# Two graph layers on one core: where the weights of later stages are loaded and prepared

## The chip, the cores and the metric

The kernel runs on 1 core of one Trainium2 chip. The metric is device time in microseconds, lower is better. The core has a matrix engine (TensorE, PE in the profile), a vector engine (VectorE, DVE), an engine for activation functions (ScalarE, ACT), GpSimd (POOL) and SyncE (SP), which here only issues DMA transfers. ScalarE and GpSimd issue transfers too; an engine's issues stand in the profile under its queue (SPq, ACTq, POOLq).

## The reference

Two graph layers run one after the other on 16 graphs of 1024 nodes with 256 features, all in float32, each followed by a residual sum and a layer norm over the features:

```
layer 0:  h = x W                        4 heads of 64
          e[i,j] = sum over t of (adj==t+1) * (a_src[t].h[i] + a_dst[t].h[j]),  leaky_relu, masked where adj == 0
          out = relu(softmax(e) h + bias) + h;  norm over each head's 64;  x = norm(x + out)
layer 1:  n = norm(x) * gamma1 + beta1;  scores = n n^T / sqrt(32), 8 heads of 32, masked where adj <= 0
          x2 = x + softmax(scores) n
          y  = norm(x2) * gamma2 + beta2;  out = x2 + gelu(y W1 + b1) W2 + b2;  x = norm(x + out)
```

W is 256 x 256 in all, W1 256 x 1024, W2 1024 x 256. adj holds 0 and 1 here, so of the five types t only the first counts; the kernel's fast path uses that (index 0 of the last axis of a_src and a_dst) and keeps a verdict whether its assumptions held.

## The kernel before, in words

Layer 0 of batch b has two stages. `prepare` (L286) takes the 1024 nodes in four pairs of blocks of 128: x is transposed on TensorE (`transpose_rows`, L222), the adjacency is transposed and turned into a mask (`turn_mask`, L290), and each block is multiplied by `w0e` (L322). `w0e` holds W and, beside it, 8 columns W a_src and W a_dst, so that one product gives h and both attention terms. ScalarE takes the product out of PSUM (L323 to L327), and VectorE adds the bias (`take_h`, L347). `attention0` (L350) then runs 16 steps: each has VectorE compute four weight tiles p (L374) and TensorE 32 products with them (L389; a float32 product gives two records). The tiles p lie in 4 buffers, two of them used by one step, and step i+1's p are computed beside step i's products. Every second head, `spread_factor` (L357; products L363, ScalarE L365) makes the factors cb for the next heads. After each head, `after0` (L432) divides and, after the last head of a half of 512 rows, runs the norms as a chain of short pieces. Layer 1 is `attention1` (L502), `finish1` and `mlp` (L629), which uses `w1_sb`, `w2_sb` and `b1_sb`.

The order on TensorE, ScalarE, VectorE and GpSimd is written out by hand for the main part (`manual_schedule`, L760): two generators, `layer0()` and `layer1()`, are advanced in turn. Each `yield` states a cost, which moves a clock; chains (`begin(chain, wait)`) are resumed when the clock reaches their time, and `complete(chain)` runs one to its end. The clock only fixes the order of instructions; the hardware then runs each engine's list in that order, with waits on semaphores. A batch of layer 1 begins when layer 0 of that batch is handed over. SyncE isn't among the engines ordered by hand: the framework orders its issues by itself, and it did so in the head of the program (before L760) for all engines.

The head, L111 to L193: constants; `w0e` is loaded by ScalarE's queue in 8 pieces (L141); then for a_src and for a_dst, one after the other, the vector is loaded into a buffer that both share (L148; 640 KB, as every partition gets a copy), multiplied by W on VectorE (L154) and summed over each head (L155) into w0e. After these, ScalarE's queue loads columns (L165), rows spread over all partitions (L159: biases, norm weights, b2), and w1, w2 and b1 (L178, L180, L182; w1 and w2 1 MB each). Then the weights are prepared: b2 - beta1 (L176), w1 times beta2 on TensorE (L188, 16 products with one column each), added to b1 (L191), and w1 scaled by gamma2 (L193, twice 128x1024). Pools named one, two, three, four and six have that many buffers for each name; `ps_o` is a pool of two PSUM banks that attention 1 and the MLP also use.

Of the kernel before, what the change touches and what calls it, by code (L numbers as in the profile page):

```python
# [31 lines left out]
F32 = mybir.dt.float32  # L32
# [4 lines left out]
OP = mybir.AluOpType  # L37
# [13 lines left out]
def fast_path(  # L51
# [56 lines left out]
    ps_o = ctx.enter_context(tc.tile_pool(name="ps_o", bufs=2, space=PSUM))  # L108


    ident = const.tile([P, P], F32, name="ident")  # L111
    make_identity(nc, ident)
    identb = const.tile([P, P], BF16, name="identb")
# [29 lines left out]
    apart = [const.tile([P, H0, Q], F32, name=f"apart{g}") for g in range(GB)]  # L143
    for t in apart:
        nc.vector.memset(t, 0.0)
    for src, dst in ((a_src, w0e[:, :, D + H0 : D + 2 * H0]), (a_dst, w0e[:, :, D : D + H0])):
        a = one.tile([P, H0, HO, T], F32, name="v0")
        nc.scalar.dma_start(  # L148
            a.rearrange("p h e t -> p (h e t)"),
            bass.AP(tensor=src.tensor, offset=src.offset, ap=[[0, P], [1, H0 * HO * T]]),  # L150
        )
        for c in range(DC):
            t = two.tile([P, H0, HO], F32, name="z")
            nc.vector.tensor_mul(t, w0e[:, c, 0:D].rearrange("p (h e) -> p h e", e=HO), a[:, :, :, 0])  # L154
            nc.vector.tensor_reduce(dst[:, c, :], t, axis=mybir.AxisListType.X, op=OP.add)  # L155

    def rows(src, name):
        t = const.tile([P, D], F32, name=name)
        nc.scalar.dma_start(t, bass.AP(tensor=src.tensor, offset=src.offset, ap=[[0, P], [1, D]]))  # L159
        return t  # L160

    columns = []
    for name, src in (("g1_c", gamma1), ("be1_c", beta1), ("g2_c", gamma2), ("be2_c", beta2)):
        t = const.tile([P, DC], F32, name=name)
        nc.scalar.dma_start(t, src.rearrange("(c p) -> p c", p=P))  # L165
        columns.append(t)
    bias0_r = rows(bias0, "bias0_r")
    nbias0_r = rows(bias0, "nbias0_r")
    nc.vector.tensor_scalar(nbias0_r, nbias0_r, -1.0, None, op0=OP.mult)
    lng0_r = rows(lng0, "lng0_r")  # L170
    lnb0_r = rows(lnb0, "lnb0_r")
    g1_r = rows(gamma1, "g1_r")
    be1_r = rows(beta1, "be1_r")

    b2_r = rows(b2, "b2_r")
    nc.vector.tensor_sub(b2_r, b2_r, be1_r)  # L176
    w1_sb = const.tile([P, DC, DFF], F32, name="w1_sb")
    nc.scalar.dma_start(w1_sb, w1.rearrange("(c p) f -> p c f", p=P))  # L178
    w2_sb = const.tile([P, FC, D], F32, name="w2_sb")
    nc.scalar.dma_start(w2_sb, w2.rearrange("(c p) d -> p c d", p=P))  # L180
    b1_sb = const.tile([P, FC], F32, name="b1_sb")
    nc.scalar.dma_start(b1_sb, b1.rearrange("c p -> p c"))  # L182

    g1_c, be1_c, g2_c, be2_c = columns
    pb = ps_o.tile([P, FC], F32, name="po")
    for f in range(FC):
        for c in range(DC):
            nc.tensor.matmul(  # L188
                pb[:, f : f + 1], w1_sb[:, c, f * P : (f + 1) * P], be2_c[:, c : c + 1], start=c == 0, stop=c == DC - 1
            )  # L190
    nc.vector.tensor_add(b1_sb, b1_sb, pb)  # L191
    for c in range(DC):
        nc.vector.tensor_scalar(w1_sb[:, c, :], w1_sb[:, c, :], g2_c[:, c : c + 1], None, op0=OP.mult)  # L193


    def power(src, n, name):
# [57 lines left out]
    def advance(cost):  # L254
        clock[0] += cost
        for item in list(chains):
            if item[0] <= clock[0]:
                run(item)
# [370 lines left out]
    def mlp(b, halves):  # L629


        chunks = [(n, q) for n in range(NH) for q in range(0, BPH, GB)]

        def first(yT, q, f, hid):
            ph = ps_s.tile([P, GB * P], F32, name="ps")
            for c in range(DC):
                nc.tensor.matmul(  # L637
                    ph,
                    w1_sb[:, c, f * P : (f + 1) * P],
                    yT[:, c, q * P : (q + GB) * P],  # L640
                    start=c == 0,
                    stop=c == DC - 1,
                )
            nc.scalar.activation(hid[f // 4][:, f % 4, :], ph, AF.Gelu, bias=b1_sb[:, f : f + 1], scale=1.0)  # L644

        def second(n, q, g, hid, x1):
            k = n * BPH + q + g
            po = ps_o.tile([P, D], F32, name="po")
            for f in range(FC):
                nc.tensor.matmul(  # L650
                    po,
                    hid[f // 4][:, f % 4, g * P : (g + 1) * P],
                    w2_sb[:, f, :],
                    start=f == 0,
                    stop=f == FC - 1,
                )
            begin(last_norm(b, k, po, x1[:, q + g, :]), 1.5)

        before = []
        for n, q in chunks:  # L660
            complete(halves[n][2])
            x1, yT, _ = halves[n]
            hid = []
            for f in range(FC):
                if f % 4 == 0:
                    hid.append(three.tile([P, 4, GB * P], F32, name="hid"))
                first(yT, q, f, hid)
                if f % 2 == 1:
                    yield 1.75
                    if f < 2 * GB and before:  # L670
                        second(*before.pop(0))
                        yield 3.5
            before = [(n, q, g, hid, x1) for g in range(GB)]
        for part in before:
            second(*part)
            yield 3.5
# [42 lines left out]
    def layer1():  # L719
        for b in range(B):  # L720
            place[1][:] = b, 0.0
            seen, rinv1, mask = handed.pop(b)

            def half(n):
                finish_norms(b, n)
                return handed[b, n]

            yT = [two.tile([P, DC, HALF], F32, name="yT") for _ in range(NH)]
            halves = {}

            def done(n, o, heads):
                x1 = handed[b, n][0]
                chain = finish1(o, x1, yT[n], heads)
                halves[n] = x1, yT[n], chain
                begin(chain, 6.0)

            yield from attention1(half, mask, rinv1, done)
            yield from mlp(b, halves)
            in_range(seen)

# [15 lines left out]
    for i in range(3):  # L756
        load_adj(i)
    load_blocks(0)
    E = mybir.EngineType
    with tc.manual_schedule(engines={E.PE, E.Activation, E.DVE, E.Pool}):  # L760
        streams = [layer0(), layer1()]
        while any(streams):
            lead = streams[0] and (place[0][0] + place[0][1] / WORK0 < wanted() or not streams[1])
            which = 0 if lead else 1
            cost = next(streams[which], None)
            if cost is None:
                streams[which] = None
            else:
                place[which][1] += cost
                advance(cost)  # L770
        while chains:
            run(chains[0])
    right = const.tile([P, B * NB], F32, name="right")
    nc.vector.tensor_scalar(right, types, N / 2 + 2.0, None, op0=OP.is_lt)
    nc.vector.tensor_reduce(ok, right, axis=mybir.AxisListType.X, op=OP.min)
# [442 lines left out]
```

## Time and profile before

| | before |
|---|---|
| time, median of 3 runs | 3663.64 us (3661.22 to 3666.74) |
| span of the profiled run | 3660.5 us, mean granted TensorE clock 0.985 |
| busy PE, DVE, ACT, POOL | 94%, 82%, 59%, 11% |
| first product at L322 | starts at 36.26 us |
| first weight tile of attention 0 (L374) | starts at 63.77 us |
| first product of attention 1 (L517) | starts at 134.03 us |
| landing of w1 and w2, from their issue | 9.2 and 11.2 us |

How to read the profile: "busy" is time with at least one instruction of that engine at work. A timeline line gives start, length, engine, line, operation, what it writes and reads, shapes, a count of merged instructions, and in brackets the idle time before it and what ended that. The chain of waits goes back from the last instruction, at each step to what released it. A wait for several things is put down to the one that came last. The granted clock of TensorE is a share of full speed.

### The profile page before, as it was taken

What the parts mean: (1) busy time and instruction counts of PE and PEld (TensorE: products, weight loads), DVE (VectorE), ACT (ScalarE), POOL (GpSimd) and SP (SyncE); (2) the same over time, 40 slices, a digit from 0 to 9 for tenths busy, and PEclk for the clock granted to TensorE, in tenths of its full rate; (3) what the DMA queues carried; (4) which work ended last, traced back from release to release, by engine and by line L of the source; (5) the groups of instructions that cost most, each with busy time, mean ns of one, the idle gap of its engine ahead of it and who ended that gap; (6) DMA issues with size and microseconds to landing.
All of it is one profiled execution on the core that took longest, in us unless ns stands there. A gap on an engine that the chain in (4) does not pass through costs nothing.

```text
span 3660.5 us, 142025 instructions
## 1 busy us (share of the span) xinstructions
PE 3452.5 (94%) x64417; PEld 2304.6 (63%) x64417; DVE 2986.7 (82%) x5328; ACT 2156.0 (59%) x4732; POOL 384.5 (11%) x360
## 2 busy tenths in 40 slices
PE   5699999999999999999999999999999999999998
PEld 4458476575766757566585765757667575665846
DVE  4888788887878888788887988888788887888884
ACT  2474846647466574755747566474665747557464
POOL 0101101010110101101011010101101011010110
PEclk9799999999999999999999999999999999999999
DMA  4110201102010110201102011020101102010000
GB/s 106 28 23 16 46 6 42 18 26 36 13 41 12 33 29 14 45 7 38 23 16 46 6 40 20 26 36 13 41 12 32 31 14 45 7 38 9 16 6 14
DMA packets 77669, 97.67 MB, mean 27 GB/s; under 512 B 9088, under 2 KB 60160, under 8 KB 77056
## 3 DMA queue, kind: packets, MB, share of 16 engines
q0 software_dynamic: 18432, 33.56, 6.4%
q1 hardware_dynamic: 52736, 50.35, 4.4%
q8 instruction: 506, 8.29, 0.9%
q10 hardware_dynamic: 5888, 4.60, 0.4%
q14 instruction: 107, 0.88, 0.1%
HBM read 105.26 MB, written 16.78 MB: 33 GB/s over the span
## 4 chain that ended last, share of the span: by engine, by line
PE 63%; DVE 26%; issue 4%; ACT 3%; POOL 3%; DMA 1%; ACTq 0%; SPq 0%; DVEq 0%; POOLq 0%
PE ps L517 13%; PE po L535 10%; PE ps L637 9%; PE acc L389 9%; DVE p L528 7%; PE po L650 7%; PE po L542 6%; DVE p L374 6%; PE acc L322 3%; POOL r L198 3%; DVE st L203 2%; PE acc L295 1%; PE acc L227 1%; PE ps L363 1%; DVE mv L204 1%
## 5 line engine op out<-in xcount | busy, mean ns | idle before, releaser
L528 DVE TENSOR_TENSOR p<-p,mask 128x1024 f32<-128x1024 f32 x1024 | 1199.1, 1218 | 160.7 <-ACT p L522 156.9
L522 ACT ACTIVATE p<-ps 128x512 f32<-128x512 f32 x2048 | 1059.6, 614 | 329.6 <-PE ps L517 327.8
L517 PE MATMUL ps<-nT 32*128 32x512 f32 x4096 | 769.1, 654 | 12.6 <-ACT cb L365 10.0
L374 DVE SCALAR_TENSOR_TENSOR p<-cb,dinv,mask 128x512 f32<-128x512 f32 x1024 | 698.4, 744 | 0.5 <-ACT cb L365 0.5
L542 PEld LDWEIGHTS po<-v,p 128*32 128x32 f32 x32768 | 390.0, 110 | 334.2 <-issue 239.5
L389 PE MATMUL acc<-v,p 128*64 128x65 f32 x16384 | 556.4, 225 | 43.8 <-DVE p L374 42.7
L389 PEld LDWEIGHTS acc<-v,p 128*64 128x64 f32 x16384 | 511.5, 139 | 118.0 <-DVE p L374 65.2
L644 ACT ACTIVATE hid<-ps,b_sb 128x256 f32<-128x256 f32 x512 | 235.5, 471 | 555.4 <-PE ps L637 555.1
L535 PE MATMUL po<-p,v 128*32 128x512 f32 x2048 | 550.2, 612 | 10.4 <-DVE p L528 8.9
L535 PE MATMUL po<-p,unit 128*32 128x512 f32 x2048 | 549.5, 612 | 0.0
L637 PE MATMUL ps<-yT,w_sb 128*128 128x256 f32 x2048 | 491.6, 387 | 0.7 <-issue 0.7
L650 PE MATMUL po<-w_sb,hid 128*128 128x256 f32 x2048 | 465.0, 381 | 0.0
L650 PEld LDWEIGHTS po<-w_sb,hid 128*128 128x128 f32 x2048 | 385.4, 190 | 64.0 <-issue 11.4
L637 PEld LDWEIGHTS ps<-yT,w_sb 128*128 128x128 f32 x2048 | 376.2, 191 | 64.3 <-issue 12.2
L542 PE MATMUL po<-v,p 128*32 128x33 f32 x32768 | 387.6, 198 | 7.5 <-DVE o L584 3.1
L517 PEld LDWEIGHTS ps<-nT 32*128 32x128 f32 x4096 | 268.0, 186 | 170.8 <-issue 56.8
L535 PEld LDWEIGHTS po<-p,v 128*32 128x32 f32 x2048 | 78.7, 109 | 387.5 <-DVE p L528 204.5
L198 POOL TENSOR_TENSOR r<-v,mhalf 128x1 f32<-128x1 f32 (+1 forms) x160 | 158.1, 988 | 1009.2 <-DVE v L684 721.7
L296 ACT ACTIVATE mask<-acc,shift_c 128x1024 uint8<-128x1024 bf16 x128 | 144.3, 1127 | 44.3 <-PE acc L295 43.8
L322 PE MATMUL acc<-w0e,xT 128*128 128x264 f32 x512 | 146.2, 409 | 20.9 <-DVE hb L347 20.8
L278 POOL DMA_DIRECT2D ak<-in_adj_dram x128 | 69.7, 545 | 878.1 <-PE acc L295 864.7
L198 POOL TENSOR_TENSOR r<-v1s,mhalf 128x4 f32<-128x4 f32 x32 | 34.9, 1092 | 1132.2 <-DVE ranges L418 891.0
(116 smaller groups left out, 2929.2 us busy)
## 6 DMA issues: line engine op xcount, KB each, us to landing
ak<-in_adj_dram POOLq DMA_DIRECT2D x128, 256.0 KB, 3.9
xk<-in_x_dram SPq DMA_DIRECT2D x64, 256.0 KB, 2.8
xl<-in_x_dram SPq DMA_DIRECT2D x32, 512.0 KB, 4.0
out_dram<-z SPq DMA_DIRECT2D x128, 128.0 KB, 1.7
w_sb<-in_L_gnn_W_dram ACTq DMA_DIRECT2D x2, 1024.0 KB, 10.2
v<-in_L_gnn_a_src_dram ACTq DMA_DIRECT2D x1, 640.0 KB, 7.8
v<-in_L_gnn_a_dst_dram ACTq DMA_DIRECT2D x1, 640.0 KB, 3.8
w0e<-in_L_gnn_W_dram ACTq DMA_DIRECT2D x8, 32.0 KB, 7.3
```

Of the source, the lines that this page charges most:

```text
L198: nc.gpsimd.tensor_tensor(r, src, mhalf[:, :n], op=OP.pow)
L322: nc.tensor.matmul(ph, xT[:, c, g * P : (g + 1) * P], w0e[:, c, :], start=c == 0, stop=c == DC - 1)
L374: nc.vector.scalar_tensor_tensor(p[:, i, :], cb[:, hd % PAIR, :], dinv[:, j2 + i, hd : hd + 1], mask[n][:, j2 + i, :], op0=OP.max, op1=OP. ...
L389: nc.tensor.matmul(av[at : at + TILE, q, :], ps[i // 2][:, i % 2, q * P + at : q * P + at + TILE], v0[:, j4 + i, hd, :], start=j4 + i == 0 ...
L517: nc.tensor.matmul(tiles[e], of_keys[q, quad, keys], of_queries[q, quad, :], start=True, stop=True)
L522: nc.scalar.activation(p[:, i, :], tiles[e + i], AF.Exp, scale=SCALE1)
L528: nc.vector.tensor_mul(p, p, mask[n][:, jb, None, :].to_broadcast([P, PAIR, HALF]))
L535: nc.tensor.matmul(moved[at * Q : (at + 1) * Q, :], v, ps[0][:, e, :], start=jb == 0, stop=jb == NB - 1)
L542: nc.tensor.matmul(held[at : at + Q, q, e, :], ps[1][:, e, q * P + at : q * P + at + Q], values[:, hd, :], start=jb == 0 and e == 0 and q ...
L637: nc.tensor.matmul(ph, w1_sb[:, c, f * P : (f + 1) * P], yT[:, c, q * P : (q + GB) * P], start=c == 0, stop=c == DC - 1,)
L644: nc.scalar.activation(hid[f // 4][:, f % 4, :], ph, AF.Gelu, bias=b1_sb[:, f : f + 1], scale=1.0)
L650: nc.tensor.matmul(po, hid[f // 4][:, f % 4, g * P : (g + 1) * P], w2_sb[:, f, :], start=f == 0, stop=f == FC - 1,)
```

## The change

The weights that only layer 1 and the end of layer 0 need are no longer loaded by ScalarE's queue in the head, but by SyncE, and what is computed from them becomes a chain, `later_weights`, that is begun with the first batch and runs in pieces beside it; `complete(weights_of_later)` stands ahead of the MLP as a safeguard. The order by hand now starts at the beginning of the program, so the head too is in program order on the four engines. The attention vectors no longer share one buffer one after the other: their four halves (two heads each) lie in the buffers of `v0` and `xl`, which nothing else needs yet; a_src is loaded by SyncE and a_dst by ScalarE. The multiplication by W is done for two heads at a time. The bias row is loaded once, and its negative computed from it. What it is for: the first batch should not wait for weights of later stages, nor a_dst for a_src.

```diff
--- before.py
+++ after.py
@@ -108,6 +108,10 @@
     ps_o = ctx.enter_context(tc.tile_pool(name="ps_o", bufs=2, space=PSUM))
 
 
+    E = mybir.EngineType
+    ctx.enter_context(tc.manual_schedule(engines={E.PE, E.Activation, E.DVE, E.Pool}))
+
+
     ident = const.tile([P, P], F32, name="ident")
     make_identity(nc, ident)
     identb = const.tile([P, P], BF16, name="identb")
@@ -143,54 +147,76 @@
     apart = [const.tile([P, H0, Q], F32, name=f"apart{g}") for g in range(GB)]
     for t in apart:
         nc.vector.memset(t, 0.0)
-    for src, dst in ((a_src, w0e[:, :, D + H0 : D + 2 * H0]), (a_dst, w0e[:, :, D : D + H0])):
-        a = one.tile([P, H0, HO, T], F32, name="v0")
-        nc.scalar.dma_start(
-            a.rearrange("p h e t -> p (h e t)"),
-            bass.AP(tensor=src.tensor, offset=src.offset, ap=[[0, P], [1, H0 * HO * T]]),
-        )
+    terms = ((a_src, nc.sync, w0e[:, :, D + H0 : D + 2 * H0]), (a_dst, nc.scalar, w0e[:, :, D : D + H0]))
+
+    at = one.tile([P, 3, PAIR, HO, T], F32, name="v0")
+    vectors = [at[:, i, :, :, :] for i in range(3)] + [one.tile([P, PAIR, HO, T], F32, name="xl")]
+    for i, (src, queue, _) in enumerate(terms):
+        for pair in range(H0 // PAIR):
+            queue.dma_start(
+                vectors[i * PAIR + pair].rearrange("p h e t -> p (h e t)"),
+                bass.AP(
+                    tensor=src.tensor,
+                    offset=src.offset + pair * PAIR * HO * T,
+                    ap=[[0, P], [1, PAIR * HO * T]],
+                ),
+            )
+
+    def rows(queue, src, name):
+        t = const.tile([P, D], F32, name=name)
+        queue.dma_start(t, bass.AP(tensor=src.tensor, offset=src.offset, ap=[[0, P], [1, D]]))
+        return t
+
+    bias0_r = rows(nc.scalar, bias0, "bias0_r")
+    for i, (_, _, dst) in enumerate(terms):
         for c in range(DC):
             t = two.tile([P, H0, HO], F32, name="z")
-            nc.vector.tensor_mul(t, w0e[:, c, 0:D].rearrange("p (h e) -> p h e", e=HO), a[:, :, :, 0])
+            for pair in range(H0 // PAIR):
+                heads = slice(pair * PAIR, (pair + 1) * PAIR)
+                nc.vector.tensor_mul(
+                    t[:, heads, :],
+                    w0e[:, c, pair * P : (pair + 1) * P].rearrange("p (h e) -> p h e", e=HO),
+                    vectors[i * PAIR + pair][:, :, :, 0],
+                )
             nc.vector.tensor_reduce(dst[:, c, :], t, axis=mybir.AxisListType.X, op=OP.add)
-
-    def rows(src, name):
-        t = const.tile([P, D], F32, name=name)
-        nc.scalar.dma_start(t, bass.AP(tensor=src.tensor, offset=src.offset, ap=[[0, P], [1, D]]))
-        return t
-
-    columns = []
-    for name, src in (("g1_c", gamma1), ("be1_c", beta1), ("g2_c", gamma2), ("be2_c", beta2)):
-        t = const.tile([P, DC], F32, name=name)
-        nc.scalar.dma_start(t, src.rearrange("(c p) -> p c", p=P))
-        columns.append(t)
-    bias0_r = rows(bias0, "bias0_r")
-    nbias0_r = rows(bias0, "nbias0_r")
-    nc.vector.tensor_scalar(nbias0_r, nbias0_r, -1.0, None, op0=OP.mult)
-    lng0_r = rows(lng0, "lng0_r")
-    lnb0_r = rows(lnb0, "lnb0_r")
-    g1_r = rows(gamma1, "g1_r")
-    be1_r = rows(beta1, "be1_r")
-
-    b2_r = rows(b2, "b2_r")
-    nc.vector.tensor_sub(b2_r, b2_r, be1_r)
+    nbias0_r = const.tile([P, D], F32, name="nbias0_r")
+    nc.vector.tensor_scalar(nbias0_r, bias0_r, -1.0, None, op0=OP.mult)
+
+    lng0_r, lnb0_r, g1_r, be1_r, b2_r = [
+        const.tile([P, D], F32, name=name) for name in ("lng0_r", "lnb0_r", "g1_r", "be1_r", "b2_r")
+    ]
+    g1_c, be1_c, g2_c, be2_c = [const.tile([P, DC], F32, name=name) for name in ("g1_c", "be1_c", "g2_c", "be2_c")]
     w1_sb = const.tile([P, DC, DFF], F32, name="w1_sb")
-    nc.scalar.dma_start(w1_sb, w1.rearrange("(c p) f -> p c f", p=P))
     w2_sb = const.tile([P, FC, D], F32, name="w2_sb")
-    nc.scalar.dma_start(w2_sb, w2.rearrange("(c p) d -> p c d", p=P))
     b1_sb = const.tile([P, FC], F32, name="b1_sb")
-    nc.scalar.dma_start(b1_sb, b1.rearrange("c p -> p c"))
-
-    g1_c, be1_c, g2_c, be2_c = columns
-    pb = ps_o.tile([P, FC], F32, name="po")
-    for f in range(FC):
+
+    def later_weights():
+        for t, src in ((lng0_r, lng0), (lnb0_r, lnb0), (g1_r, gamma1), (be1_r, beta1), (b2_r, b2)):
+            nc.sync.dma_start(t, bass.AP(tensor=src.tensor, offset=src.offset, ap=[[0, P], [1, D]]))
+        for t, src in ((g1_c, gamma1), (be1_c, beta1), (g2_c, gamma2), (be2_c, beta2)):
+            nc.sync.dma_start(t, src.rearrange("(c p) -> p c", p=P))
+        nc.sync.dma_start(b1_sb, b1.rearrange("c p -> p c"))
+        yield 6.0
+        nc.sync.dma_start(w1_sb, w1.rearrange("(c p) f -> p c f", p=P))
+        nc.sync.dma_start(w2_sb, w2.rearrange("(c p) d -> p c d", p=P))
+        yield 24.0
+
+        nc.vector.tensor_sub(b2_r, b2_r, be1_r)
+
+        pb = ps_o.tile([P, FC], F32, name="po")
+        for f in range(FC):
+            for c in range(DC):
+                nc.tensor.matmul(
+                    pb[:, f : f + 1],
+                    w1_sb[:, c, f * P : (f + 1) * P],
+                    be2_c[:, c : c + 1],
+                    start=c == 0,
+                    stop=c == DC - 1,
+                )
+        yield 3.5
+        nc.vector.tensor_add(b1_sb, b1_sb, pb)
         for c in range(DC):
-            nc.tensor.matmul(
-                pb[:, f : f + 1], w1_sb[:, c, f * P : (f + 1) * P], be2_c[:, c : c + 1], start=c == 0, stop=c == DC - 1
-            )
-    nc.vector.tensor_add(b1_sb, b1_sb, pb)
-    for c in range(DC):
-        nc.vector.tensor_scalar(w1_sb[:, c, :], w1_sb[:, c, :], g2_c[:, c : c + 1], None, op0=OP.mult)
+            nc.vector.tensor_scalar(w1_sb[:, c, :], w1_sb[:, c, :], g2_c[:, c : c + 1], None, op0=OP.mult)
 
 
     def power(src, n, name):
@@ -735,6 +761,7 @@
                 begin(chain, 6.0)
 
             yield from attention1(half, mask, rinv1, done)
+            complete(weights_of_later)
             yield from mlp(b, halves)
             in_range(seen)
 
@@ -756,20 +783,20 @@
     for i in range(3):
         load_adj(i)
     load_blocks(0)
-    E = mybir.EngineType
-    with tc.manual_schedule(engines={E.PE, E.Activation, E.DVE, E.Pool}):
-        streams = [layer0(), layer1()]
-        while any(streams):
-            lead = streams[0] and (place[0][0] + place[0][1] / WORK0 < wanted() or not streams[1])
-            which = 0 if lead else 1
-            cost = next(streams[which], None)
-            if cost is None:
-                streams[which] = None
-            else:
-                place[which][1] += cost
-                advance(cost)
-        while chains:
-            run(chains[0])
+    weights_of_later = later_weights()
+    begin(weights_of_later, 3.0)
+    streams = [layer0(), layer1()]
+    while any(streams):
+        lead = streams[0] and (place[0][0] + place[0][1] / WORK0 < wanted() or not streams[1])
+        which = 0 if lead else 1
+        cost = next(streams[which], None)
+        if cost is None:
+            streams[which] = None
+        else:
+            place[which][1] += cost
+            advance(cost)
+    while chains:
+        run(chains[0])
     right = const.tile([P, B * NB], F32, name="right")
     nc.vector.tensor_scalar(right, types, N / 2 + 2.0, None, op0=OP.is_lt)
     nc.vector.tensor_reduce(ok, right, axis=mybir.AxisListType.X, op=OP.min)
```

## The prediction

> **What bounds the kernel now.** I read the page first, then the chain that ended last in order of time for the first 140 us, then the timeline of the same stretch, and last the sums by stage and the waits. The page says which engine carries the whole run:
>
> ```profile
> span 3660.5 us, 142025 instructions
> ...
> PE 3452.5 (94%) x64417; PEld 2304.6 (63%) x64417; DVE 2986.7 (82%) x5328; ACT 2156.0 (59%) x4732; POOL 384.5 (11%) x360
> ...
> PE 63%; DVE 26%; issue 4%; ACT 3%; POOL 3%; DMA 1%; ACTq 0%; SPq 0%; DVEq 0%; POOLq 0%
> ```
>
> TensorE bounds the body, and the change shortens nothing there. It touches the head, where little else can run: layer 1 needs layer 0 of batch 0, which needs the product at L322. So a microsecond off the start of the first L322 moves all later work by as much, unless it is given back. The chain of the first stretch (start, length, what):
>
> ```profile
> 1.78 10.14 DMA xl<-in_x_dram
> ...
> 18.05 2.03 ACTq L159
> 20.12 9.24 DMA w_sb<-in_L_gnn_W_dram
> 29.41 6.99 PE po L188 x32
> 36.40 1.98 PE acc L322 x4
> ```
>
> The last wait before the first L322 is the load of w1 (9.24 us), then the 16 products at L188 (32 matmul records, 6.99 us). L322 uses neither; they are merely ahead of it on TensorE. The timeline of the same stretch shows when its own inputs were there:
>
> ```profile
> 1.78 0.46 SPq L269 DMA_DIRECT2D xl<-in_x_dram  x1
> ...
> 6.11 0.69 ACTq L148 DMA_DIRECT2D v<-in_L_gnn_a_src_dram  x1
> ...
> 15.25 0.35 ACTq L148 DMA_DIRECT2D v<-in_L_gnn_a_dst_dram  x1
> ...
> 19.11 1.14 DVE L154 TENSOR_TENSOR z<-w0e,v 128x256 f32<-128x256 f32 x2 [3.11 <-DMA v<-in_L_gnn_a_dst_dram]
> ...
> 24.14 1.28 ACT L230 ACT_TABLE_LOAD   x1 [24.14 <-DMA lnb_r<-in_L_gnn_ln_beta_dram]
> ...
> 36.26 2.11 PE L322 MATMUL acc<-w0e,xT 128*128 128x264 f32 x4
> ```
>
> w0e was complete at 20.9 us (L154 from 19.11, L155 to 20.91), ScalarE computed nothing before 24.14 because it was still issuing loads, and L322 started at 36.26. Sums of two stretches (us, PE, PEld, DVE, ACT, POOL, clock, DMA share, GB/s):
>
> ```profile
> 5.00:10.00 5.00, 0.00 (x0) 0.10 (x1) 0.00 (x0) 0.00 (x0) 0.00 (x0) 1.00 1.00 213
> 64.00:112.00 48.00, 39.16 (x908) 31.05 (x908) 47.58 (x91) 4.42 (x8) 0.00 (x0) 1.00 0.01 3
> ```
>
> Before 14 us the DMA engines are the limit. From 64 to 112 us, attention of layer 0 for batch 0, VectorE is (47.58 of 48 us) and TensorE has 9 us free: that is where the moved work lands.
>
> **What the Trainium skill says.** "DMA: Bandwidth & Descriptors", section "Issuing engines are not separate DMA queues": loads from any engine share the same 16 DMA engines and interleave. The trace agrees: share 1.00 from 5 to 10 us with three issuers. So moving loads to SyncE frees ScalarE's time, but the bytes ahead of L322 decide. "TensorE: Matmul & The Clock Gate", Part 1: the array runs at half clock until it has been busy for a window of about 3.4 us, and falls back after an idle one. Here the same two L322 products took 2.11 us at 36.26 and 1.16 us from 40.12 on, so the head runs cold; the records also show clock 0.59 from 120 to 140 us, after TensorE pauses.
>
> **The change, part by part.**
> *w1, w2, rows, columns and b1 leave ScalarE's queue; L188, L191, L193 and L176 leave the head.* Removed from the path: all between w0e being ready and L322. What remains:
> 1. Bytes. Up to the landing of a_src at 13.9 us (6.11 + 7.8 to landing), w0e 0.26 MB, xk 2 x 0.26, xl 0.52, ak 3 x 0.26 and a_src 0.66 had been asked for: 2.75 MB. The rates of the windows (162, 213, then 232 GB/s) give 2.78 MB by then, so this is bandwidth. After the change both vectors must be there (2 x 0.66), and xl can't be fetched early, since its buffer holds half of a_dst: 2.89 MB, landing at 13.9 + 0.14/0.232 = 14.5 us. Loads behind them on SyncE mix in. SyncE isn't in the hand-written order (the xl load of a much later step went out at 1.78), so rows and w1, w2 will go out early too, whatever the place of their chain. None of it mixed in: 14.5. The five rows wholly ahead (0.66 MB): 17.3. w1 and w2 too (2.1 MB at 252 GB/s): 25.6. I take 15, since a_dst sits in ScalarE's queue near its front and w1, w2 are SyncE's last.
> 2. VectorE after that landing: for a_dst two chunks of two half multiplies and a reduce. A half is not in the trace; the whole L154 is 609 ns and a 128x64 operation (L421) 276, so 276 to 609; I take 350. 2 x (2 x 350 + 409) = 2.2 us.
> 3. ScalarE issues 8 + 2 + 1 loads; with waits for earlier landings until 11 to 12 us, then 1.3 for the table and 1.7 for xT and the first mask: ready at 15, hidden behind 17.
>
> So L322 starts at 15 + 2.2 = 17.2 instead of 36.26: 19.1 us less (bounds 14.5 + 1.7 and 25.6 + 2.9: from 20.1 to 7.8 less).
> *The second bias load* (0.13 MB) goes; the negation (282 ns) waits for the one left, hidden behind ScalarE's L323 to L327, for which VectorE waits anyway (up to 3.4 us at L347).
> *The prepared weights come back inside attention 0.* By the yields (13 for prepare, 1 + 1, then 2 a step) the chain, due 24 after 9.75, runs at clock 35, after step 9; its last part at 39. VectorE gets L176 424 + L191 155 + 2 x 751 = 2.1 us, all on the path, as VectorE has no gap there. TensorE gets L188: 6.99 us cold, and 3.5 if the warm clock halves it. Behind it on TensorE stand these (products, spread factors), and VectorE waits for the buffers that they free:
>
> ```profile
> 96.87 2.67 PE L389 MATMUL acc<-v,p 128*64 128x65 f32 x64 [1.42 <-DVE p L374]
> ...
> 99.47 1.13 PE L363 MATMUL ps<-esr,spread 32*128 32x512 f32 x4
> ```
>
> Step 9 ends at 95.44. With L188, then two steps of 2.0 us and 1.13 for L363, TensorE is through step 11 at 104.1 to 107.6, and VectorE, which has the 2.4 us of L445 and L446 to do here, needs those buffers at about 108.5; the factor (cb) for step 12 is wanted at 105.6 and comes at 103.2 to 106.7. So 0 to 1.1 us; I take 0.3.
> *w1 and w2 beside prepare* (2.1 MB, 8 us of DMA in some 26) slow the loads of adj and x; prepare runs at a DMA share of 0.65 and ScalarE is its bound (16.36 of 20 us), with adj three blocks ahead. 0 to 3 us; I take 0.2.
> Sum: -19.1 + 2.1 + 0.3 + 0.2 = -16.5 us; 3663.6 - 16.5 = 3647.
>
> **Rivals.**
> *A, the loads collide.* w1 and w2 get ahead of a_dst, and L322 starts near 26 (-10.3), with 2.1 + 1 given back: about -7, 3657. For it: SyncE fetches greedily, and loads wait for landings of unrelated ones:
>
> ```profile
> SPq L269 <- DMA w0e<-in_L_gnn_W_dram: 10.4, 1, 10.4
> ```
>
> A load of x there waited for w0e, because (so the records) eight completion semaphores go round among all loads of SyncE and ScalarE. Against it: that same rule holds w1 back until the ninth load before it or so has landed.
> *B, the hand-over warms up.* From 129.9 to 166 us some 16 us of TensorE work on the chain ran at half clock. If the shifted pauses let it run warm, up to 8 us more: 3639. Against it: the pauses come from VectorE's chain and shift with it.
> *C, slower.* L322 near 28 (-8), prepare cold throughout for want of L188's burst (12.73 us of TensorE in 20 would become 25, so 26 us become 33: +7), x blocks stuck behind w1 and w2 in SyncE's queue (+5), 2.1 + 1 given back: +7, 3671. Against it: a TensorE that is full when cold warms itself, and L188 for 7 us didn't warm it either (L322 after it was cold).
>
> **How the numbers follow.** Main case 0.68, A 0.12, B 0.14, C 0.06. The time is that of the main case, 3647. Its own bounds (L322 from 16.2 to 20.2, prices) give 3645 to 3651, a few us more for clock windows and for the spread of the runs before (3661 to 3667). With part of A and B the range is 3638 to 3656. 0.2% is 7.3 us, so faster means below 3656.3: main and B nearly whole, a third of A: 0.86; same 0.08; slower 0.06.
>
> **What would show it.** First L322 at 16 to 20 us, with VectorE's multiply of a_dst as its releaser. ScalarE's table load near 12. L188 near 76 us, between two L389 groups, taking 3.5 to 7 us with no gap on VectorE behind it; VectorE's work of attention 0 longer by 2.1. The first L517 at about 117.5 instead of 134.03, and the rest of the timeline the same distance ahead. It is wrong if L322 waits for a_dst beyond 22, if prepare takes over 28 us, or if the gap at the first L517 differs from that at the end.

## The result, and the profile after

| | before | after |
|---|---|---|
| time, median of 4 runs | 3663.93 us (3661.22 to 3666.74) | 3648.76 us (3646.30 to 3652.41) |
| ratio to before, 95% interval | | 0.9959 (0.9942 to 0.9977) |
| span of the profiled run | 3660.5 us | 3649.4 us |
| first product of W and x done (ScalarE's first copy out of it) | 38.40 | 21.48 |
| first weight tile of attention 0 | 63.77 | 46.87 |
| first product of attention 1 | 134.03 | 119.36 |

The kernel is 15.2 us faster; 3647 us had been forecast. Lines have moved: L322 is now L348, L188 L209, L374 L400, L389 L415, L517 L543, L154 L176. The page of the profile after, its totals and shares of the chain:

```profile
span 3649.4 us, 142033 instructions
...
PE 3449.4 (95%) x64417; PEld 2302.3 (63%) x64417; DVE 2988.7 (82%) x5332; ACT 2155.9 (59%) x4732; POOL 384.4 (11%) x360
...
PE 64%; DVE 25%; issue 4%; ACT 3%; POOL 3%; DMA 1%; SPq 0%; ACTq 0%; POOLq 0%; DVEq 0%
```

Busy times are those of before to some 3 us: nothing was saved in work, only in waiting. The chain of waits in order of time (start, length, what) for the head and the place where the prepared weights come back:

```profile
0.76 4.32 DMA w0e<-in_L_gnn_W_dram
5.10 7.79 DMA w0e<-in_L_gnn_W_dram
12.90 5.33 DMA xl<-in_L_gnn_a_dst_dram
...
73.22 5.32 PE acc L415 x128
78.55 4.77 PE po L209 x32
83.32 3.66 PE acc L415 x64
86.98 1.48 PE ps L389 x4
88.49 0.61 ACT cb L391
```

w1 (9.24 us) and L188 (6.99 us) are gone from the head. In their place stands a_dst, and ahead of it W. The timeline of the same stretch:

```profile
9.56 0.33 ACTq L156 DMA_DIRECT2D v<-in_L_gnn_a_dst_dram  x1
...
12.90 0.33 ACTq L156 DMA_DIRECT2D xl<-in_L_gnn_a_dst_dram  x1
...
14.06 1.28 ACT L256 ACT_TABLE_LOAD   x1 [14.06 <-DMA v<-in_L_gnn_a_dst_dram]
...
18.25 0.39 DVE L176 TENSOR_TENSOR z<-w0e,xl 128x128 f32<-128x128 f32 x1 [3.33 <-DMA xl<-in_L_gnn_a_dst_dram]
...
18.72 0.51 SPq L295 DMA_DIRECT2D xk<-in_x_dram  x1
...
19.20 2.25 PE L348 MATMUL acc<-w0e,xT 128*128 128x264 f32 x4 [8.52 <-issue]
19.28 0.47 SPq L200 DMA_DIRECT2D w_sb<-in_L_gnn_W_dram  x1
```

The second half of a_dst was issued only at 12.90, when the sixth piece of W had landed, and was there at 18.24. L348 began at 19.20 with the part of w0e that was ready and waited inside for the last reduce. SyncE sent the third x load just ahead of w1 here. And the place of the prepared weights, with VectorE's only wait of that stretch:

```profile
78.48 4.84 PE L209 MATMUL po<-be_c,w_sb 128*128 128x1 f32 x32
...
83.25 3.73 PE L415 MATMUL acc<-v,p 128*64 128x65 f32 x64
...
89.12 2.74 DVE L400 SCALAR_TENSOR_TENSOR p<-cb,dinv,mask 128x512 f32<-128x512 f32 x4 [0.40 <-ACT cb L391]
```

### The profile page after: what moved, and what is told of

The parts are those of the page before. It is cut to its first block, busy times and chain, and to the rows that moved or that the text cites. A ratio compares the mean times of both kernels' runs of the same rounds, so it can differ in the third digit from the quotient of the medians.

```text
span 3649.4 us, 142033 instructions
## 1 busy us (share of the span) xinstructions
PE 3449.4 (95%) x64417; PEld 2302.3 (63%) x64417; DVE 2988.7 (82%) x5332; ACT 2155.9 (59%) x4732; POOL 384.4 (11%) x360
## 3 DMA queue, kind: packets, MB, share of 16 engines
q10 hardware_dynamic: 1584, 1.05, 0.1%
## 4 chain that ended last, share of the span: by engine, by line
PE 64%; DVE 25%; issue 4%; ACT 3%; POOL 3%; DMA 1%; SPq 0%; ACTq 0%; POOLq 0%; DVEq 0%
PE ps L543 13%; PE po L561 10%; PE ps L663 9%; PE acc L415 9%; DVE p L554 7%; PE po L676 7%; PE po L568 6%; DVE p L400 6%; PE acc L348 3%; POOL r L224 3%; DVE st L229 2%; PE acc L321 1%; PE acc L253 1%; PE ps L389 1%; DVE mv L230 1%
## 5 line engine op out<-in xcount | busy, mean ns | idle before, releaser
L543 PE MATMUL ps<-nT 32*128 32x512 f32 x4096 | 770.1, 655 | 12.6 <-ACT cb L391 10.0
L400 DVE SCALAR_TENSOR_TENSOR p<-cb,dinv,mask 128x512 f32<-128x512 f32 x1024 | 698.5, 744 | 0.9 <-ACT cb L391 0.9
L415 PE MATMUL acc<-v,p 128*64 128x65 f32 x16384 | 556.1, 226 | 42.1 <-DVE p L400 40.1
L415 PEld LDWEIGHTS acc<-v,p 128*64 128x64 f32 x16384 | 512.0, 139 | 114.3 <-DVE p L400 61.6
L561 PE MATMUL po<-p,v 128*32 128x512 f32 x2048 | 548.3, 610 | 10.5 <-DVE p L554 8.8
L543 PEld LDWEIGHTS ps<-nT 32*128 32x128 f32 x4096 | 268.2, 186 | 171.1 <-issue 56.9
L348 PE MATMUL acc<-w0e,xT 128*128 128x264 f32 x512 | 146.4, 409 | 29.5 <-DVE hb L373 20.9
L322 ACT ACTIVATE mask<-acc,shift_c 128x1024 uint8<-128x1024 bf16 x128 | 144.3, 1127 | 43.6 <-PE acc L321 42.8
```

Source lines behind the costliest of these rows:

```text
L348: nc.tensor.matmul(ph, xT[:, c, g * P : (g + 1) * P], w0e[:, c, :], start=c == 0, stop=c == DC - 1)
L400: nc.vector.scalar_tensor_tensor(p[:, i, :], cb[:, hd % PAIR, :], dinv[:, j2 + i, hd : hd + 1], mask[n][:, j2 + i, :], op0=OP.max, op1=OP. ...
L415: nc.tensor.matmul(av[at : at + TILE, q, :], ps[i // 2][:, i % 2, q * P + at : q * P + at + TILE], v0[:, j4 + i, hd, :], start=j4 + i == 0 ...
L543: nc.tensor.matmul(tiles[e], of_keys[q, quad, keys], of_queries[q, quad, :], start=True, stop=True)
L561: nc.tensor.matmul(moved[at * Q : (at + 1) * Q, :], v, ps[0][:, e, :], start=jb == 0, stop=jb == NB - 1)
```

## Experiments

All stages below are read in one profile per run: "product" is ScalarE's first copy out of the first product of W and x, "tile" VectorE's first weight tile, "attention 1" TensorE's first product of it. The time from product to tile is prepare, from tile to attention 1 attention 0; the body is from there to TensorE's last product.

| run | median us | ratio to before (95%) | product | tile | attention 1 | prepare | attention 0 | body |
|---|---|---|---|---|---|---|---|---|
| before | | | 38.40 | 63.77 | 134.03 | 25.4 | 70.3 | 3518 |
| the change | 3648.76 | 0.9959 (0.9942-0.9977) | 21.48 | 46.87 | 119.36 | 25.4 | 72.5 | 3522 |
| the change, again | 3650.54 | 0.9963 (0.9951-0.9975) | 24.67 | 52.40 | 124.38 | 27.7 | 72.0 | 3515 |
| the change, third | 3652.39 | 0.9962 (0.9948-0.9976) | 23.69 | 51.41 | 123.89 | 27.7 | 72.5 | 3522 |
| weights only | 3659.51 | 0.9988 (0.9981-0.9994) | 31.84 | 57.26 | 129.73 | 25.4 | 72.5 | 3518 |
| buffers only | 3664.52 | 1.0001 (0.9993-1.0010) | 39.12 | 64.49 | 134.75 | 25.4 | 70.3 | 3515 |
| no products | 3662.20 | 0.9992 (0.9984-1.0001) | 22.91 | 50.63 | 122.55 | 27.7 | 71.9 | 3531 |
| other products | 3652.57 | 0.9956 (0.9941-0.9971) | 23.68 | 49.08 | 121.51 | 25.4 | 72.4 | 3522 |
| products at start | 3652.86 | 0.9957 (0.9942-0.9973) | 24.02 | 50.38 | 122.32 | 26.4 | 71.9 | 3521 |
| type 0 alone | 3654.68 | 0.9967 (0.9955-0.9979) | 22.63 | 48.02 | 120.49 | 25.4 | 72.5 | 3521 |
| W in two loads | 3646.17 (one run) | | 16.88 | 46.43 | 118.43 | 29.6 | 72.0 | 3518 |
| all of it | 3650.48 | 0.9954 (0.9940-0.9967) | 14.83 | 44.40 | 115.59 | 29.6 | 71.2 | 3520 |
| late loads | 3650.56 | 0.9956 (0.9942-0.9969) | 18.02 | 46.70 | 118.70 | 28.7 | 72.0 | 3520 |
| all, late | 3646.69 | 0.9942 (0.9928-0.9956) | 15.09 | 42.80 | 113.12 | 27.7 | 70.3 | 3523 |

Beside the first pair, the runs come from two chips. The medians of before on them were 3664.38 (again, weights only, buffers only, no products) and 3667.16 to 3667.97 (the rest), so times are compared by their ratios. Runs of one kernel spread over 5 to 7 us; differences of a few microseconds are read in the stages, not in the totals.

### The two halves of the change apart

Weights only: the vectors share one buffer again, each in one load on ScalarE's queue. The order by hand from the start of the program and the single load of the bias row stay as in the change; what these two do was not tried apart.

```diff
-    at = one.tile([P, 3, PAIR, HO, T], F32, name="v0")
-    vectors = [...]
...
+    for src, _, dst in terms:
+        a = one.tile([P, H0, HO, T], F32, name="v0")
+        nc.scalar.dma_start(a.rearrange("p h e t -> p (h e t)"), ...)
```

> The later weights moved as in the change, but a_src and a_dst still share one buffer, one load each on ScalarE's queue, multiplied for all heads at once. My theory: most of the gain is that TensorE no longer stands behind w1; a_src lands near 13 us, is used until 15, a_dst then takes 4 to 8 us beside the rows and w1: first product (L348 or its line here) complete near 23 to 26, so 2 to 5 us less gain than the change: about -10 to -13 us against before. Rival (own buffers do most): a gain of under 6 us.

Buffers only: the kernel before, with the loads and multiplications of the vectors from the change.

> Own buffers alone: the kernel before with the vectors loaded and multiplied as in the change, all else in the head as it was. My theory: w1 still stands ahead of the first product, so nothing or 1 to 2 us: the first product at 34 to 36 us. Rival (the vectors bound the head): 5 us or more of gain.

Measured: moving the weights alone gives 4.9 us, own buffers alone nothing, both together 14 to 16. The expected 10 to 13 for the first was wrong. Its chain, and the issue of a_src from its timeline, show why:

```profile
4.65 10.16 DMA w0e<-in_L_gnn_W_dram
15.26 4.36 DMA be_c<-in_L_gnn_beta_dram
...
21.26 7.17 DMA v<-in_L_gnn_a_dst_dram
29.62 2.19 PE acc L334 x4
```

```profile
14.44 0.33 ACTq L160 DMA_DIRECT2D v<-in_L_gnn_a_src_dram  x1
```

a_src was issued only at 14.44, behind the pieces of W, and VectorE could begin with it at 19.64. (The chain puts this wait down to be_c, a column that lands at about the same time; the multiplication reads a_src and not be_c.) a_dst needed a_src's buffer, so it was issued at 21.26, when the multiplications were over, and then took 7.17 us. Two loads of the vectors, one after the other, took the place of the wait for w1 and L188. With buffers only, the chain is that of before: 6.42 us for w1 at 23.59, then 6.96 for L188, and the product where it was. Each half removes one of two waits that lie side by side, and only the pair pays in full.

### What sets the landing of a_dst: bytes or semaphores

Type 0 alone loads a fifth of both vectors (128 KB instead of 640 KB each).

```diff
-        laid[name] = laid[name].transpose(0, 2, 1)
+        laid[name] = laid[name].transpose(1, 0, 2)
...
+    at = one.tile([P, 2, H0, HO], F32, name="v0")
+        queue.dma_start(at[:, i, :, :]..., bass.AP(tensor=src.tensor, offset=src.offset, ap=[[0, P], [1, H0 * HO]]))
```

> The changed kernel, but a_src and a_dst are laid out with the type first, and only type 0, which is all that the fast path uses, is loaded: 128 KB each instead of 640 KB. My theory (bytes ahead of a_dst and the eight semaphores that go round set the head): a_dst and w0e land near 10 us, the first product is done at 13 to 15 us instead of 21.5 to 24.7, so 7 to 10 us earlier, and the end moves by as much: about 3640 to 3643. Rival (something else in the head bounds, such as ScalarE's issues or the load of x): under 3 us earlier.

The product was done at 22.63, no earlier than in the change (21.48 to 24.67), with 1.05 MB less ahead of it. The expected 13 to 15 was wrong. The chain:

```profile
2.71 9.43 DMA w0e<-in_L_gnn_W_dram
12.15 7.34 DMA v<-in_L_gnn_a_dst_dram
```

a_dst was issued at 12.15, the moment the fifth piece of W had landed. In the trace the two loads carry the same completion semaphore: eight of them go round among the loads of SyncE and ScalarE, and each load waits until the one that had its semaphore before has landed. The 128 KB of a_dst then took 7.34 us among rows and columns from SyncE. So W was cut differently:

```diff
-        for h in range(H0):
-            nc.scalar.dma_start(w0e[:, c, h * HO : (h + 1) * HO], w0[h, c * P : (c + 1) * P, :])
+        nc.scalar.dma_start(w0e[:, c, 0:D]..., w0[:, c * P : (c + 1) * P, :].rearrange("h p e -> p h e"))
```

> The changed kernel with W in two loads of 128 KB instead of eight of 32 KB, all else as it is: 13 fewer-by-six loads ahead of a_dst, the same bytes. Semaphore theory: a_dst is issued near 2 us instead of 9.6 and 12.9, and lands as the bytes allow, at 12 to 15; product done at 15 to 18. Bytes theory: lands at 17 to 18 as before.

The product was done at 16.88, with the same bytes: six loads fewer ahead of a_dst are worth 4.6 to 7.8 us. (This is one run with one profile.) a_dst was issued early, as expected, and VectorE multiplied by its second half when it had landed:

```profile
1.80 0.53 ACTq L157 DMA_DIRECT2D v<-in_L_gnn_a_dst_dram  x1
2.36 0.45 ACTq L157 DMA_DIRECT2D xl<-in_L_gnn_a_dst_dram  x1
...
13.65 0.39 DVE L177 TENSOR_TENSOR z<-w0e,xl 128x128 f32<-128x128 f32 x1 [2.14 <-DMA xl<-in_L_gnn_a_dst_dram]
```

So the bytes do count: a load issued at 2.36 still landed only at 13.65, near the 14.5 that the prediction had reckoned for the bytes when nothing mixes in. The wait for semaphores and the rows and columns that mix in come on top; in the three profiles of the change they added 3.7 to 6.9 us. The late loads below show what the rows and columns do: with the eight pieces of W kept and SyncE's rows and columns gone, a_dst was issued at 8.55 and 10.01, and VectorE began with its second half at 14.79.

But the tile came at 46.43, almost where it was in the first profile of the change (46.87; 52.40 and 51.41 in the two others). The chain of this run shows what ate it:

```profile
12.04 1.21 ACT mask L323 x2
13.26 1.34 issue
14.60 2.26 PE acc L349 x4
...
23.75 12.15 DMA xk<-in_x_dram
36.05 1.10 PE acc L254 x4
```

The fourth load of x, in SyncE's queue behind w1 (21.38) and w2 (21.93), took 12.15 us to land, and TensorE had no x to transpose: prepare took 29.6 us. This is the wait that rival C had named ("x blocks stuck behind w1 and w2"). In the change itself the fourth load goes out behind them too (24.84), but the block is wanted only at 37.67, 4.4 us later than here (36.05 less a wait of 2.75), and the load had landed by then: the chain has no wait for x there.

### The version with everything

"All of it" joins type 0 alone, W in two loads, and the preparation on idle engines:

```diff
-        nc.vector.tensor_sub(b2_r, b2_r, be1_r)
+        nc.gpsimd.tensor_sub(b2_r, b2_r, be1_r)
...
-            nc.vector.tensor_scalar(w1_sb[:, c, :], w1_sb[:, c, :], g2_c[:, c : c + 1], None, op0=OP.mult)
+            nc.scalar.mul(w1_sb[:, c, :], w1_sb[:, c, :], g2_c[:, c : c + 1])
```

> As the run with type 0 alone, and also W in two loads instead of eight (fewer loads, so fewer waits for an earlier landing), w1 scaled by ScalarE and b2 - beta1 by GpSimd, which are idle there, instead of VectorE. My theory: 1 to 3 us more off the head, and 1.9 us off VectorE in attention 0: the first L543 some 3 to 5 us before that run's, 3636 to 3640. Rival: the head is bound by x and adj now, and VectorE's 1.9 us were hidden: no difference to that run.

The product came at 14.83, and attention 1 began 4.9 us before the run with type 0 alone, as expected. The time, 3650.48, missed the expected 3636 to 3640; the intervals of the two ratios overlap. Attention 0 was 1.3 us shorter, but prepare took 29.6 us. TensorE waited 1.54 us for the second block of adj and 2.01 for the third load of x, and then ran cold again (2.13 us at L337, 30.24). SyncE, ordered by the framework, had put w1 ahead of that load of x (in the change it is the other way round):

```profile
20.68 0.54 SPq L189 DMA_DIRECT2D w_sb<-in_L_gnn_W_dram  x1
21.33 0.40 SPq L284 DMA_DIRECT2D xk<-in_x_dram  x1
21.78 0.47 SPq L190 DMA_DIRECT2D w_sb<-in_L_gnn_W_dram  x1
```

So the later loads were given to GpSimd, whose order is written by hand, and begun after prepare; first on the change alone, then on top of everything.

```diff
-            nc.sync.dma_start(...)
+            nc.gpsimd.dma_start(...)
-        yield 24.0
+        yield 14.0
...
-    begin(weights_of_later, 3.0)
+    begin(weights_of_later, 14.0)
```

> The changed kernel with the loads of later_weights issued by GpSimd, whose order is written by hand, and begun after prepare (clock 14 and 20 instead of 3.25 and 9.75); the prepared weights come at the same clock 35. Nothing of the later weights can then mix with the head's loads or hold a semaphore that they wait for. Theory (rows, columns and b1 mixed in by SyncE delay a_dst): the second half of a_dst lands near 15 instead of 18.2 to 21.4 us, the first product is done at 17 to 19; -3 us against the changed kernel at the first weight tile. Rival (W's eight pieces alone hold a_dst back): product at 21 or later.

> The same late loads by GpSimd on top of the run with everything (type 0 alone, W in two loads, weights prepared by ScalarE and GpSimd). There the product was done at 14.8, but prepare took 29.6 us, since the third x load was issued behind SyncE's later weights (21.33) and adj landed after 14 us. Theory: product at 12 to 14, prepare back at 25.4 to 27, first weight tile at 38 to 40 (44.4 in that run, 46.9 to 52.4 in the changed kernel), attention 0 71.2, the first L543 near 110; time about 18 to 25 us under before. Rival (the head's gains don't reach the end, as the body varies): within 2 us of the changed kernel.

> The changed kernel unaltered beside these, on the same chip: 0.995 to 0.9965 of before; product done between 21 and 25 us, prepare 25.4 when TensorE's clock rises before 25 us and some 2 us more when it rises after 30.

Late loads alone brought the product forward to 18.02 (expected 17 to 19), so the rival, W's pieces alone, fell. The tile came at 46.70: 4.7 us before the change on the same chip (51.41), but hardly before its first profile (46.87), since prepare ran cold: TensorE got its full clock only at 32.2 us. With everything and late loads the product was done at 15.09 (a little later than expected, adj's landing at 11.8 now being the wait), the tile at 42.80 and attention 1 at 113.12 (expected near 110; prepare was 2.3 us longer than warm). Attention 0 took 70.32, as before the change (70.27): with w1's scaling on ScalarE (2.18 us, idle there) and the subtraction on GpSimd, the 2.2 us that the change put on VectorE are gone. ("All of it" has the same two edits and took 71.2; there the clock fell to half at 77.9, inside TensorE's burst of products, and here only after it.) Beside the change on the same chip: 3646.69 (3642.27 to 3648.62) against 3652.39 (3651.03 to 3657.65). It is 21 us under before, as expected. No run of one reaches the other's range, though the intervals of the two ratios overlap a little. It is the fastest of those timed in several runs. The change itself came out as expected (0.9962, product at 23.69).

### TensorE's products among the attention

> The changed kernel without TensorE's 16 products of w1 and beta2 and without adding them to b1 (this part of the MLP's bias is left out). My theory: TensorE's 4.8 us lie in its free time, VectorE waits only 0.4 us behind them and spends 0.15 on the addition: the first L543 comes 0.4 to 0.8 us earlier than in the changed kernel. Rival (the burst lowers the clock and delays the stage): 2 us or more earlier, and no half-clock stretch near 81 us.

```diff
-        pb = ps_o.tile([P, FC], F32, name="po")
-        for f in range(FC):
-            for c in range(DC):
-                nc.tensor.matmul(pb[:, f : f + 1], w1_sb[...], be2_c[...], ...)
...
-        nc.vector.tensor_add(b1_sb, b1_sb, pb)
```

In the stage it did about as expected: attention 0 took 71.9 us instead of 72.0 to 72.5, and TensorE had its full clock from 33.0 to 104.7 us. A part of the rival is real, but small: with the products, attention 0 took 72.4 to 72.5 us in the five profiles where the clock fell inside their burst (the change, its third, weights only, other products, type 0 alone), and 72.0 in the three where it fell after it or not at all (again, W in two loads, late loads). But the whole ran 11 us slower than the change on the same chip (3662.20 against 3650.54). The loss is spread over the body (3531 us, against 3515 to 3523 in all others). Two more runs put 16 products that nothing reads back in, once in the same place and once at the start of the program:

```diff
+                nc.tensor.matmul(pb[:, f : f + 1], ident, unit[:, c : c + 1], start=c == 0, stop=c == DC - 1)
```

> As the run without products, with 16 products of the same shape in their place that read constants and are not used (that part of the MLP's bias is still left out). That run was 11 to 13 us slower than the changed kernel though it does less. If the place of the later instructions in TensorE's stream does it (32 records fewer ahead of them, so its supply of instructions pauses elsewhere), or if the burst itself does, this one is back at 3648 to 3652. If it is chance of the clock windows or the data, it stays near 3660.

> The same 16 unused products at the start of the program, where TensorE waits for x (that part of the MLP's bias is left out as well). All later instructions of TensorE then stand at the same place of its stream as in the changed kernel, but no burst lies in attention 0. Position theory: 3646 to 3652, with few pauses by issue in the body (about 4 to 6 us, against 9 in the run without products). Burst theory: near 3660.

Both are back (0.9956 and 0.9957). So it isn't the burst in attention 0, since the second has none there. The number of TensorE's instructions ahead of the body fits, but it is not shown to be the cause, for a rival was not tried: the run without products also takes one buffer fewer from `ps_o`, whose two banks are handed out in turn, so that all later results in that pool should lie in the other bank of the two; both runs with unused products take that buffer. Waits of TensorE from 200 to 3540 us that nothing in the profile explains ("issue": total us, times, longest), in the run without products, whose lines stand 11 lower:

```profile
PE po L557 <- issue: 6.1, 13, 0.8
PE acc L404 <- issue: 3.0, 6, 0.7
```

with the products at the start:

```profile
PE po L562 <- issue: 2.7, 6, 0.6
PE acc L409 <- issue: 2.4, 6, 0.8
PE ps L657 <- issue: 0.6, 1, 0.6
```

and in the first profile of the change:

```profile
PE po L568 <- issue: 4.3, 7, 1.0
PE acc L415 <- issue: 2.0, 4, 0.9
PE ps L663 <- issue: 0.4, 1, 0.4
```

These pauses make up 9.1 us against 5.7 and 6.7, so they are a part of the loss at most. The clock records of the body add to it: 22 half-clock windows of 3.4 us, against 17 to 20 in all other runs. Why the pauses and the windows were more numerous there stays open.

### The same kernel again

> The changed kernel once more, to see how much of the gain at the first product of attention 1 (14.67 us in the first pair of profiles) is left at the end. My theory: the head's gain is the same again to 1 us (first L543 at 119 to 120 us), and what is lost later (3.6 us in the first profile) comes from half-clock windows and small pauses of TensorE that fall elsewhere in each run, so it will differ: ratio to before 0.995 to 0.997. Rival: the changed order costs something in every batch; then the same loss of 3 to 5 us shows again, at the same batches.

The expected 119 to 120 us for the head was wrong: attention 1 began at 124.38 and, in the third profile, at 123.89. Two things differ between runs of one program. The second half of a_dst took 9.01 us to land instead of 5.33 (issued at 12.40 instead of 12.90), and the array stayed cold for longer: full clock from 33.8 and 34.2 us in the two later profiles, not from 22.8. The second group of L348 in the two profiles, first the change, then again:

```profile
23.22 1.16 PE L348 MATMUL acc<-w0e,xT 128*128 128x264 f32 x4 [0.92 <-DVE hb L373]
```

```profile
26.41 2.13 PE L348 MATMUL acc<-w0e,xT 128*128 128x264 f32 x4 [0.92 <-DVE hb L373]
```

Cold, prepare took 27.7 us. What decides it can be read from all fourteen profiles. The half-clock records last 3.4 us or a multiple of it, and the last 3.4 us before the full clock began held TensorE busy for 78 to 100%. A cold prepare keeps it busy for only about 73% (2.48 of 3.40 us, twice, from 23.6 to 30.4 us in the run again), and such stretches did not raise the clock. (One of 82%, in late loads, didn't raise it either, so no sharp bound can be read off.) In the first profile the stretch from 19.4 to 22.8 was busy for 2.90 us, and the clock rose after it. Where the first product falls among these stretches differs from run to run. Prepare goes with the time from the first product to the full clock, wherever x and adj were there in time: it took 25.4 us when that was 0.9 to 1.6 us (before, the change, and four others), 26.4 at 5.0, 27.7 at 9.2 to 10.5 (four profiles), and 28.7 at 14.2. The clock's own time doesn't matter: with weights only it rose at 33.1 us, right after the product, and prepare took 25.4.

The end doesn't follow the head closely: the run that was 5 us later at attention 1 ended 2 us earlier, since its body was 7 us shorter. Set side by side, instruction by instruction, the two profiles of the change drift apart at half-clock windows that only one of them has (1.2 to 1.6 us each where TensorE is the bound) and at pauses of half a microsecond. The lead over the profile of before, at the first product of attention 1 in batches 1, 5, 9 and 13 and at the end, was 14.7, 11.1, 10.1, 10.1 and 11.1 us in the first profile, 9.7, 9.5, 10.9, 11.5 and 13.2 in the second, and 10.1, 10.0, 9.1, 7.7 and 7.4 in the third. The loss in the first profile after attention 1 is scatter of the body, not a cost of the new order: one of the others gains, and the one that loses does so in other batches. The rival, the same loss at the same batches, fell.

## Why the prediction was right

It named the mechanism and the sum: 16.5 us less was forecast, 15.2 measured. By its steps:

- **L188 and w1 leave the path of the first product.** Right, with a condition that the prediction took as given: without own buffers it is worth only 4.9 us.
- **Landing of a_dst: 15, from 14.5 for the bytes to 25.6.** Measured 18.24 and 21.41 in the first two profiles and 20.43 in the third. That is inside the bounds, but the 0.5 us taken for what comes on top of the bytes was too small; it was 3.7 to 6.9. The 14.5 for the bytes alone was good (13.65 with W in two loads, 14.79 with late loads). What was missed is the wait for semaphores: a megabyte less changed nothing, and six loads fewer moved the product 4.6 us or more. The rule of the eight semaphores stood in the prediction, but only as an argument about w1; it should have been applied to ScalarE's own queue, where the eight pieces of W stood ahead of a_dst.
- **VectorE after that: 2.2 us, 350 ns for a half.** Measured 1.9 (18.25 to 20.14); a half takes 390 ns, but some of the work was done before the landing.
- **First L322 at 17.2 instead of 36.26 (-19.1).** The start moved by 17.06 us (19.20), the end of the product by 16.92 in the first profile, by 13.7 and 14.7 in the others. This is the mis-sized term, by 2.2 to 5.4 us, and it follows from a_dst's landing.
- **ScalarE ready at 15.** It was at 17.0 (mask done), still ahead of the product.
- **Prepared weights: 2.1 us of VectorE, 0.3 of waiting.** Attention 0 grew by 2.2, 1.7 and 2.2 us; VectorE waited 0.40 at L400 for cb. Without TensorE's products it grew by 1.65; with the weights prepared on other engines and late loads by nothing. So most of it was VectorE's work, and up to 0.5 the half clock during the burst.
- **L188 (now L209) in 3.5 to 7 us.** It took 4.84.
- **Prepare 0.2 us longer.** 0.0 in the first profile, 2.3 in the two others. w1 and w2 cost nothing there; the cold TensorE did, which the prediction had put into rival C. That ScalarE bounds prepare, as read from the profile before, holds only at full clock.
- **Rivals.** B didn't come (hand-over and attention 0 together no faster). A's collision is real in a mild form: rows and columns held a_dst's semaphores and bandwidth. C's stuck x load appears as soon as a_dst no longer hides it, and the argument against its cold prepare, that a full TensorE warms itself, did not hold: cold, it was busy for 73% and stayed cold for 9 to 14 us in five profiles.
- **The signs.** ScalarE's table load came at 14.06 instead of near 12, and attention 1 at 119.36 to 124.38 instead of 117.5. One of the three signs of being wrong did show: the lead at attention 1 (14.7) differs from that at the end (11.1), which is the scatter above. Another showed in the second profile alone: L348 began at 22.38, where 22 was the limit.

That the total came so close to 3647 is partly luck: the head gave 9.7 to 14.7 us in three profiles, and the body of one program varies by 7 us. In the first profile the head gave 1.8 us less than forecast at attention 1 (14.7 instead of 16.5), and the time still came within 1.3 us.

## What to carry to other kernels

When loads share a few completion semaphores in rotation, count loads as well as bytes: with eight semaphores, even a small load waits until the load about eight places ahead of it has landed, whichever queue that one is in. Moving loads to a queue that the framework orders doesn't place them in time; if they should be late, issue them from an engine whose order is written by hand, or they may get ahead of what is urgent, as w1 did ahead of x. And when two waits lie side by side, try the removals together before judging either.

## What was not expected of the hardware

- The array's clock fell to half in the middle of a dense burst: L209 ran from 78.48 to 83.32 and the half-clock record begins at 80.9 (6.8 us long), so the next L415 group took 3.73 us instead of the 2.67 at 96.87 before. The Trainium skill ("TensorE: Matmul & The Clock Gate", Part 1) has the clock follow how busy the array was in windows of about 3.4 us; TensorE was busy for all of the 3.4 us before 80.9, and for 2.4 of them with L209. So it looks as if products with a single moving column, though back to back, do not count as busy. In the ten profiles that have such a burst in attention 0, the clock fell inside it in six, within 1 us after it in three, and not at all in one (late loads, 78.3 to 82.0), so the reading is likely rather than shown. The head before agrees: L188 filled 29.41 to 36.40, and the clock rose only at 39.96, after L322 had begun.
- In the body, the half-clock windows follow 3.4 us in which TensorE was busy for 30 to 70%. The pauses in them are only 2.3 us (ahead of the transposes at L253) or 1.9 us (ahead of L415); the half clock then lasts 3.4 us and costs 1.2 to 1.6 where TensorE is the bound.
- Leaving out 32 TensorE instruction records ahead of the body, and the PSUM buffer that they write, made a program of 3650 us 11 us slower; 32 that do nothing useful, into such a buffer, made it fast again. Which of the two matters is open.
